# One engine per transposed block, identity products and one PSUM pool at the seam between image attention and the output stage

## The chip, the cores and the metric

The kernel runs on one core of one Trainium2 chip, in float32 throughout. The metric is the device time of one execution in microseconds (us). The engines are TensorE (PE, with its weight loads shown as PEld), VectorE (DVE), ScalarE (ACT), GpSimd (POOL) and SyncE (SP), which here only issues transfers. PE writes its results to PSUM, eight banks of 512 float32 values in each of 128 partitions; DVE and ACT copy them out from there to SBUF.

## The reference

Four layers, each applied to a group-normed copy of a tensor of 4 x 56 x 56 x 128 and added to it. Layers 0 and 1 are window and global attention with an MLP, and an edge layer. The change lies in layer 2, which treats every sample as a set of images, with an attention between them and spectral convolutions in each:

```python
x = x + _L0_conv_ref(_gn(x), ...)          # window attention, attention, MLP
x = x + _L1_conv_ref(_gn(x), ...)          # edge layer
x = x + _L2_conv_ref(_gn(x), ...)          # image attention and spectral layers
x = x + _L3_conv_ref(_gn(x), L3_conv_W, L3_conv_b)

# in layer 2
k = _fno_layer(xa_n, wK, wKs, bKs, (H // 2, W // 2))
q = _fno_layer(xa_n, wQ, wQs, bQs, (H // 2, W // 2))
v = _fno_layer(xa_n, wV, wVs, bVs, (H, W))
scores = jnp.einsum('bhtd,bhsd->bhts', qs, ks) / (np.sqrt(ks.shape[-1]) * TEMPERATURE)
attn_w = jax.nn.softmax(scores, axis=-1)
out = jnp.einsum('bhts,bhsd->bhtd', attn_w, vs)
projd = _fno_layer(out, wP, wPs, bPs, (H, W))
attention = _inorm(projd + xa, norm_g[1], norm_b[1])
an = _inorm(attention, norm_g[2], norm_b[2])
m = _fno_layer(an, wM0, wM0s, bM0s, (H, W), (norm_g[3], norm_b[3]), act=True)
m = _fno_layer(m, wM1, wM1s, bM1s, (H, W), (norm_g[4], norm_b[4]), act=False)
output = _inorm(m, norm_g[5], norm_b[5]) + attention
```

Here `_fno_layer` is a truncated two-dimensional Fourier transform, a product per mode, the inverse transform and a skip path, and `_inorm` normalizes an image.

## The kernel before

The whole computation is one program. Layers 0 and 1 run sample by sample (4 samples) until about 2700 us of the profile; then come the spectra and the score weights of layer 2, the image attention in `attend`, and the output stage in `outputs`, which does the rest of layer 2 and layer 3.

`attend` (L1802) works through 24 turns (g, n, bp): four groups g of eight spectral columns, three parts n of a complex product, two pairs bp of samples. In each turn DVE and POOL multiply a spectrum by coefficients (`u_ud`, `u_up`), PE multiplies with the attention weights `AT` into a bank `u_po` (L1874), and the result is copied or added into `st.y`, which has for each bp 32 columns c, each of 128 partitions (two samples of 64 images) by 2 x 56 values. After the last turn, two additions on DVE (L1901) finish the columns 24 to 31 of bp = 1. Those of bp = 0 are finished one turn earlier. `attend` holds its own PSUM pool: two buffers `u_px` of two banks, one `x_po` of two banks (for a part called `mix_images` and for the last softmax) and two of one bank for `u_po`.

`outputs` (L2630) opens a PSUM pool of its own: three buffers `o_d` of two banks each (`banks()`, tag d) and two `o_b` of one bank (`bank()`, tag b). A new pool gets the memory of the closed one, and work in it waits for what the old pool's buffers are still used for. The stage is described as a list of operations (`plan.add`), numbered in the order in which they are added, and issued in the order of the hand-written list OUTPUT_ORDER (L2598). Each engine takes its own instructions in that order. A sample is worked on in two halves of 28 images; (sample, half) is a unit, and two samples, so four units, share a bp.

`attended_rows` (L2569) is the seam. For each bp it turns the 32 columns of `st.y` in four blocks of eight: eight transpositions on PE into one `o_d` buffer (L2586), then four copies (L2593), one per unit, into the unit's rows `o_y` (112 partitions, 28 images, 32 columns). The copies of units with an odd number in the pair go to DVE, the others to ACT, so both engines read every block. Operations 0 to 19 are the four blocks of bp = 0 (0, 5, 10, 15 are the transpositions, for columns 0, 8, 16, 24; the four numbers after each are the copies), operations 20 to 39 those of bp = 1. The second group stands in the middle of the stage, after the first two samples have begun.

A unit then goes on in `half_sample` (L2067): `put_dc` (L2265, ACT) writes one row into `o_y`; `over_h` (L2114, PE) multiplies the rows with a transform, seven products a unit; `plain` (L2272, ACT) copies; `over_c` (L2131, PE) goes on; an addition (L2281, DVE) adds `o_a`, which SP has loaded from memory (L2260, four loads of 784 KB at the start of the stage); `over_w` (L2145), `weighted` (L2167, PE, then L2174, DVE) and so on, with norms and a gelu (L2336, ACT) between. `last_layer` does layer 3 per sample. The input of a sample for the last sums, `o_x`, is loaded (L2347) into memory that `st.y` leaves, so once all its rows are turned; `constant` (L2357, ACT) is the first to use it. `before_x`, the list of all copies, orders this load.

In the list, `put_dc` names all 16 copies of its bp and the load of `o_a` as operations that have to be issued before it. The waits on the chip are made from the buffers that the instructions touch, not from the list.

Of the kernel before, what the change touches and what calls it, by code (L numbers as in the profile page):

```python
# [12 lines left out]
F32 = mybir.dt.float32  # L13
# [3 lines left out]
PSUM = bass.MemoryType.PSUM  # L17
DRAM = bass.MemoryType.DRAM

P = 128  # L20
# [1780 lines left out]

def attend(k, I, w, st, dd, xat, xm, softmax, beside):  # L1802

    nc, tc = k.nc, k.tc
    with ExitStack() as es:
        mk = es.enter_context(tc.tile_pool(name="x_wk", bufs=1))
        dk = es.enter_context(tc.tile_pool(name="u_dk", bufs=3))
        wk = es.enter_context(tc.tile_pool(name="u_wk", bufs=2))  # L1810
        psum = es.enter_context(tc.tile_pool(name="u_ps", bufs=2, space=PSUM))

        def bank():
            return psum.tile([P, 2, 512], F32, name="x_po", bufs=1)

# [6 lines left out]
        def prepare(turn):  # L1822
            if turn == len(turns):
                return
            g, n, bp = turns[turn]
# [13 lines left out]
            else:  # L1839

                x, re = (st.xh[:, bs, i, cs, :].rearrange("p b c r -> p b (c r)") for i in (1, 0))
                nc.gpsimd.tensor_add(x, re, x)
            px = psum.tile([112, 2, 512], F32, name="u_px")
            nc.scalar.copy(px[:, :, :NB], x)
# [13 lines left out]
        for turn, (g, n, bp) in enumerate(turns):  # L1858
            cs = slice(8 * g, 8 * g + 8)
            x, px = ready.pop(turn)  # L1860
            po = psum.tile([P, 512], F32, tag="acc", name="u_po")
            left = 16
# [204 lines left out]
def half_sample(k, w, st, plan, b, half, whole, pools, rows, x2d, xm):  # L2067
# [4 lines left out]
    nc = k.nc  # L2072
    wk, psum = pools.wk, pools.psum
    T, G = HH // 2, HH // 8
# [12 lines left out]
    def bank():  # L2087
        return psum.tile([P, 512], F32, tag="b", name="o_b", bufs=2)

    def banks():  # L2090
        return psum.tile([P, 2, 512], F32, tag="d", name="o_d", bufs=3)

# [4 lines left out]
    def op(engine, cost, after=(), takes=(), gives=(), **kw):  # L2097
        return lambda run: plan.add(engine, cost, run, after, takes, gives, **kw)
# [162 lines left out]

    @op("ACT", 0.2, rows.ops + [load_a])
    def put_dc():
        V.y = rows.y[me]
        nc.scalar.copy(V.y[0:1, :, 0], st.dc[:, b, t0:t0 + T])  # L2265
# [169 lines left out]
def last_layer(k, w, plan, b, whole, pools, out):  # L2435


    nc = k.nc
    wk, psum = pools.wk, pools.psum
    V = Env()  # L2440
    count = [0]

    def buf(n):
        count[0] += 1
        return n, (b, count[0])

    def bank():
        return psum.tile([P, 512], F32, tag="b", name="o_b", bufs=2)

    def banks():  # L2450
        return psum.tile([P, 2, 512], F32, tag="d", name="o_d", bufs=3)

# [116 lines left out]
def attended_rows(k, st, plan, bp, pools):  # L2569

    nc = k.nc
    T = HH // 2
    rows = Env()
    rows.y, rows.ops, first = {}, [], []
    units = [(2 * bp + b2, half) for b2 in range(2) for half in range(2)]
    for c0 in range(0, 32, 8):
        d = "d", ("rows", bp, c0)
        L = Env()

        def turn(c0=c0, L=L):  # L2580
            if c0 == 0:
                for u in units:
                    rows.y[u] = pools.wk.tile([112, T, 32], F32, tag="y0", name="o_y0", bufs=4)
            L.pt = pools.psum.tile([P, 2, 512], F32, tag="d", name="o_d", bufs=3).rearrange("p i (c t) -> p (i c) t", c=4)
            for c in range(8):
                nc.tensor.transpose(L.pt[:112, c, :], st.y[:, bp, c0 + c].rearrange("p i r -> p (i r)"), k.ident)  # L2586
        p = plan.add("PE", 1.8, turn, first, [d] + ([("y0", u) for u in units] if c0 == 0 else []))
        first = first or [p]
        for i, (b, half) in enumerate(units):
            def copy_rows(i=i, b=b, half=half, c0=c0, L=L):  # L2590
                o = rows.y[b, half][:, :, c0:c0 + 8].rearrange("p t c -> p c t")
                at = 64 * (b % 2) + T * half
                (nc.vector.tensor_copy if i % 2 else nc.scalar.copy)(o, L.pt[:112, :, at:at + T])  # L2593
            rows.ops.append(plan.add("DVE" if i % 2 else "ACT", 0.4, copy_rows, [p], (), [d]))
    return rows


OUTPUT_ORDER = """  # L2598
# [30 lines left out]

def outputs(k, w, st, ys, x2d, xm, out):  # L2630

    tc = k.tc
    with ExitStack() as es:
        pools = Env()
        pools.wk = es.enter_context(tc.tile_pool(name="o_wk", bufs=2))
        pools.psum = es.enter_context(tc.tile_pool(name="o_ps", bufs=2, space=PSUM))
        opened = []

# [48 lines left out]
def build(k, packs, I, out):  # L2687
# [3 lines left out]
    with ExitStack() as es:  # L2691
# [100 lines left out]
        with tc.tile_pool(name="xh", bufs=1) as xp:  # L2792
            st.xh = xp.tile([112, B, 2, 32, HH], F32, name="xh")
            with tc.tile_pool(name="sp", bufs=1) as sp:
# [43 lines left out]
```

## Time and profile before

The time before is the median of three runs, 3626.33 us (3609.95 to 3628.69). The profile is of another execution.

| | value |
|---|---|
| time of the profiled execution | 3623.46 us |
| its span | 3621.7 us |
| mean granted TensorE clock | 0.973 |
| instructions | 80884 |
| attention products u_po (L1874), first to last | 2923.7 to 3253.6 us |
| output stage, first transposition to the end | 3255.4 to 3621.7 us |
| transpositions (L2586), records on PE | 64, of 272 ns each (median) |
| row copies (L2593) on ACT and on DVE | 16 of 552 ns and 16 of 534 ns (medians) |
| put_dc (L2265) | 8 of 232 ns |
| over_h (L2114), records on PE | 336, of 275 ns each (median) |
| last additions to y (L1901) | 2 of 618 ns |

How to read it: the page sums each engine's busy time over the span; the chain of waits follows the work that ended last back to the start, and gives each piece to an engine and a line. The timeline lists instructions of an engine with start, busy time, and in brackets how long the engine had been idle before and what ended that. A matmul's record is longer than its distance to the next, since matmuls are pipelined: the busy time of a row of them, divided by their number, says what one costs in a row. The windows sum busy time in stretches, with the granted clock of TensorE as a share of full speed. Transpositions and products carry one `MATMUL` and one `LDWEIGHTS` record or more each.

### The profile page before, as it was taken

To read this page: it belongs to the slowest core of one execution; us is meant where nothing else is said; L and a number is where in the kernel's file an instruction comes from. 1 tells how busy PE (TensorE), PEld (TensorE's weight loads), DVE (VectorE), ACT (ScalarE), POOL (GpSimd) and SP (SyncE) were. 2 spreads that over 40 slices of the span, in tenths; PEclk is the share of its full clock that TensorE was granted. 3 is DMA by queue.
4 is the path that set the end of the run, shared out by engine and by line. 5 is a ranking of instruction groups with operands and counts; after the bars stand their busy time and mean duration, and the time that the engine had idled before them with its cause. 6 is when DMAs were issued, how large, how long until landed. Compare 5 with 4: busy or idle time off the path is not lost.

```text
span 3621.7 us, 80884 instructions
## 1 busy us (share of the span) xinstructions
PE 3401.0 (94%) x36096; PEld 1567.0 (43%) x36096; DVE 2706.0 (75%) x2532; ACT 2091.6 (58%) x2103; POOL 1247.4 (34%) x751
## 2 busy tenths in 40 slices
PE   6999998999999898999989899999898989999998
PEld 4433344553333455333346543334466433336664
DVE  6588859758887786788859658885965768885756
ACT  4688865458887555788856468886542012215432
POOL 1000018500000660000038200001854768874766
PEclk9999999999999999999999999999998999999989
DMA  2243320024442002344400034332021047742201
GB/s 102 48 92 87 91 41 20 20 57 92 93 92 62 20 3 54 76 95 96 93 19 3 20 87 93 87 88 53 26 66 33 1 108 187 181 107 79 63 10 54
DMA packets 98496, 244.51 MB, mean 68 GB/s; under 512 B 64540, under 2 KB 69916, under 8 KB 93244
## 3 DMA queue, kind: packets, MB, share of 16 engines
q0 software_dynamic: 16128, 102.77, 14.0%
q1 hardware_dynamic: 75152, 123.61, 11.6%
q10 hardware_dynamic: 6860, 12.88, 1.3%
q8 instruction: 285, 4.67, 0.5%
q14 instruction: 71, 0.58, 0.0%
HBM read 79.46 MB, written 31.33 MB: 31 GB/s over the span
## 4 chain that ended last, share of the span: by engine, by line
PE 78%; DVE 10%; ACT 4%; issue 4%; POOL 3%; DMA 0%; DVEq 0%; POOLq 0%; SPq 0%; ACTq 0%
PE f_pm L818 17%; PE f_pm L684 15%; PE u_po L1874 8%; PE e_acc L1238 7%; PE q_acc L1732 3%; DVE e_td L1231 3%; PE f_pm L791 2%; PE e_po L1206 2%; PE f_pm L770 2%; ACT f_ring L821 1%; PE o_d L2548 1%; PE f_pm L464 1%; PE o_d L2145 1%; DVE f_acc L673 1%; PE f_pm L715 1%
## 5 line engine op out<-in xcount | busy, mean ns | idle before, releaser
L821 ACT ACTIVATE f_ring<-f_pm 128x1792 f32<-128x1792 f32 (+1 forms) x764 | 1093.9, 1482 | 228.6 <-PE f_pm L818 181.1
L673 DVE TENSOR_TENSOR f_acc<-f_acc,f_ring 128x1792 f32<-128x1792 f32 x468 | 947.7, 2025 | 191.1 <-ACT f_ring L821 160.9
L818 PE MATMUL f_pm<-f_qT,f_kT 32*128 32x448 f32 x5376 | 725.1, 571 | 15.5 <-ACT f_ring L821 5.1
L684 PE MATMUL f_pm<-f_ring,f_va 128*32 128x448 f32 (+1 forms) x6304 | 589.4, 490 | 0.0
L663 POOL DMA_DIRECT2D f_far<-f_ring x112 | 96.6, 862 | 1329.4 <-ACT f_ring L821 1087.9
L1231 DVE TENSOR_TENSOR e_td<-e_pa,e_c 128x1792 f32<-128x1792 f32 x252 | 491.1, 2018 | 14.1 <-ACT e_a L1196 14.1
L1233 POOL TENSOR_TENSOR e_tp<-e_a,e_c 128x1792 f32<-128x1792 f32 x140 | 451.5, 3263 | 101.5 <-PE e_acc L1238 60.0
L818 PEld LDWEIGHTS f_pm<-f_qT,f_kT 32*128 32x128 f32 x5376 | 260.0, 183 | 417.5 <-ACT f_ring L821 305.0
L1238 PE MATMUL e_acc<-e_td,t_shared 32*32 32x448 f32 x8064 | 325.9, 544 | 24.9 <-DVE e_td L1231 24.1
L684 PEld LDWEIGHTS f_pm<-f_ring,f_va 128*32 128x32 f32 x6304 | 163.8, 109 | 410.1 <-issue 397.8
L1869 DVE TENSOR_TENSOR u_ud<-u_px,u_d 112x1792 f32<-112x1792 f32 (+1 forms) x145 | 264.9, 1859 | 43.3 <-PE u_po L1874 35.9
L1235 ACT ACTIVATE e_tp<-e_tp 128x1792 f32<-128x1792 f32 x140 | 233.4, 1694 | 74.0 <-POOL e_tp L1233 74.0
L1871 POOL TENSOR_TENSOR u_up<-xh,u_d 112x1792 f32<-112x1792 f32 (+1 forms) x71 | 238.8, 3390 | 50.4 <-PE u_po L1874 36.3
L1238 PE MATMUL e_acc<-e_tp,t_shared 32*32 32x448 f32 x4480 | 222.8, 544 | 3.1 <-ACT e_tp L1235 2.4
L1874 PE MATMUL u_po<-u_ud,AT 112*64 112x448 f32 x1060 | 218.1, 549 | 6.4 <-issue 6.4
L1238 PEld LDWEIGHTS e_acc<-e_td,t_shared 32*32 32x32 f32 x8064 | 142.2, 103 | 138.5 <-DVE e_td L1231 79.5
L1874 PEld LDWEIGHTS u_po<-u_ud,AT 112*64 112x64 f32 x1060 | 75.6, 139 | 136.8 <-issue 122.5
L1717 POOL TENSOR_TENSOR q_u<-iS,q_g 128x1792 f32<-128x1792 f32 x32 | 102.8, 3236 | 64.9 <-PE s_px L1565 41.8
L1250 ACT COPY e_sums<-e_acc 128x1792 f32<-128x1792 f32 x28 | 46.3, 1652 | 136.4 <-PE e_acc L1238 136.4
L1238 PEld LDWEIGHTS e_acc<-e_tp,t_shared 32*32 32x32 f32 x4480 | 96.7, 103 | 52.9 <-issue 16.4
L728 DVE RECIPROCAL f_den<-f_den 128x448 f32<-128x448 f32 x28 | 82.6, 2951 | 44.1 <-ACT f_den L725 44.1
L1874 PE MATMUL u_po<-u_up,AT 112*64 112x448 f32 x476 | 105.1, 554 | 9.0 <-POOL u_up L1871 9.0
(525 smaller groups left out, 4557.0 us busy)
## 6 DMA issues: line engine op xcount, KB each, us to landing
f_far<-f_ring POOLq DMA_DIRECT2D x112, 896.0 KB, 6.3
u_d<-dd SPq DMA_DIRECT2D x44, 784.0 KB
f_far<-f_ring SPq DMA_DIRECT2D x28, 896.0 KB
xw<-in_x SPq DMA_DIRECT2D x4, 1568.0 KB
x2d<-x SPq DMA_DIRECT2D x4, 1568.0 KB
xat<-x SPq DMA_DIRECT2D x4, 1568.0 KB
x_xs<-xat ACTq DMA_DIRECT2D x32, 196.0 KB
xm<-x_ev ACTq DMA_DIRECT2D x64, 98.0 KB
```

The source lines that it names most:

```text
L673: nc.vector.tensor_add(e.acc, e.acc, slots(j, c))
L684: nc.tensor.matmul(e.po[heads[h], part], va[o, c, heads[h]], p, start=(c == 0), stop=(c == 23 and part.stop == NB))
L818: nc.tensor.matmul(ss[:, i, :NB], kT[heads[h], c * P:(c + 1) * P], qT[heads[h], blk(j)], start=True, stop=True)
L821: nc.scalar.activation(ring[:, slot:slot + m, :], ss[:, :m, :NB], AF.Exp, scale=scale)
L1231: nc.vector.tensor_tensor(t, am, cm, ALU.max)
L1233: nc.gpsimd.tensor_sub(t, bc(a.rearrange("p (l n) -> p l n", l=8), 1, 4), cm)
L1235: nc.scalar.activation(tf, tf, AF.Relu)
L1238: nc.tensor.matmul(acc[quarters[q], r, :NB], k.ident[o, o], t[o, q].rearrange("p l n -> p (l n)"), start=(g == 0), stop=(g == len(EDGE_TUR ...
L1732: nc.tensor.matmul(acc[bp][i][halves[hb % 2], hb // 2, :NB], x[o], u[o, 8 * hb:8 * hb + 8, :].rearrange("p h t -> p (h t)"), start=first, ...
L1869: nc.vector.tensor_mul(u, bc(px[:, :, :NB], 2, m), dm)
L1871: nc.gpsimd.tensor_mul(u, bc(x, 2, m), dm)
L1874: nc.tensor.matmul(po[64 * b2:64 * b2 + 64, :NB], st.AT[:, 8 * i + h0 + q, 2 * bp + b2, :], u[:, b2, q, :], start=(left == 16), stop=(left ...
```

## The change

- The transpositions `nc.tensor.transpose(out, in, ident)` become products `nc.tensor.matmul(out, in, ident)` of the same operands.
- A block is copied by one engine: for bp = 0, columns 8 and 24 by DVE and 0 and 16 by ACT; for bp = 1, columns 8 and 16 by DVE and 0 and 24 by ACT.
- `put_dc` of a unit names the four copies of its own unit (`rows.of[me]`) instead of all 16.
- OUTPUT_ORDER changes in two places: the first group's blocks are issued in the order 0, 5, 10, 15, their copies in order of their numbers, and each `put_dc` (41, 120, 228, 307) and the first `over_h` (42) stand between the last copies; in the second group the copies stand in order of their numbers. Transpositions of the second group keep their places.
- One PSUM pool is opened before `attend` and passed to `attend` and `outputs`. Its tags are px (two buffers of two banks), x (one of two banks) and b (two of one bank). `banks()` of the output stage goes round px, px, x; `bank()` is b, as `u_po` is.

```diff
-def attend(k, I, w, st, dd, xat, xm, softmax, beside):
+def attend(k, I, w, st, dd, xat, xm, softmax, beside, psum):
...
-        psum = es.enter_context(tc.tile_pool(name="u_ps", bufs=2, space=PSUM))
...
-            return psum.tile([P, 2, 512], F32, name="x_po", bufs=1)
+            return psum.tile([P, 2, 512], F32, tag="x", name="x_po", bufs=1)
...
-            px = psum.tile([112, 2, 512], F32, name="u_px")
+            px = psum.tile([P, 2, 512], F32, tag="px", name="u_px")[:112]
...
-            po = psum.tile([P, 512], F32, tag="acc", name="u_po")
+            po = psum.tile([P, 512], F32, tag="b", name="u_po")
...
-    @op("ACT", 0.2, rows.ops + [load_a])
+    @op("ACT", 0.2, rows.of[me] + [load_a])
     def put_dc():
...
+        dve = c0 in ((16, 8) if bp else (8, 24))
...
-            L.pt = pools.psum.tile([P, 2, 512], F32, tag="d", name="o_d", bufs=3).rearrange("p i (c t) -> p (i c) t", c=4)
+            L.pt = pools.banks().rearrange("p i (c t) -> p (i c) t", c=4)
             for c in range(8):
-                nc.tensor.transpose(L.pt[:112, c, :], st.y[:, bp, c0 + c].rearrange("p i r -> p (i r)"), k.ident)
+                nc.tensor.matmul(L.pt[:112, c, :], st.y[:, bp, c0 + c].rearrange("p i r -> p (i r)"), k.ident, start=True,
+                                 stop=True)
...
-                (nc.vector.tensor_copy if i % 2 else nc.scalar.copy)(o, L.pt[:112, :, at:at + T])
-            rows.ops.append(plan.add("DVE" if i % 2 else "ACT", 0.4, copy_rows, [p], (), [d]))
+                (nc.vector.tensor_copy if dve else nc.scalar.copy)(o, L.pt[:112, :, at:at + T])
+            rows.ops.append(plan.add("DVE" if dve else "ACT", 0.4, copy_rows, [p], (), [d]))
+            rows.of.setdefault((b, half), []).append(rows.ops[-1])
...
-0 40 119 227 306 10 3 2 1 4 5 13 12 11 14 15 6 9 7 8 18 19 16 17 41 228 120 42 307 121 43 45 44 122 124 229 47
+0 40 119 227 306 5 10 1 2 3 4 6 7 8 9 15 11 16 41 42 12 17 120 13 18 228 14 19 307 121 43 45 44 122 124 229 47
...
-239 73 149 147 74 76 240 20 150 247 25 24 23 22 21 248 77 35 29 27 30 28 37 36 39 26 38 82 31 32 33 34 78 151 83
+239 73 149 147 74 76 240 20 150 247 25 21 22 23 24 248 77 35 26 27 28 29 30 36 37 38 39 82 31 32 33 34 78
+151 83
...
-        pools.psum = es.enter_context(tc.tile_pool(name="o_ps", bufs=2, space=PSUM))
-        opened = []
+        opened, taken = [], [0]
+
+        def bank():
+            return psum.tile([P, 512], F32, tag="b", name="o_b")
+
+        def banks():
+            taken[0] += 1
+            tag, bufs = ("x", 1) if taken[0] % 3 == 0 else ("px", 2)
+            return psum.tile([P, 2, 512], F32, tag=tag, name="o_d", bufs=bufs)
+        pools.bank, pools.banks = bank, banks
...
-            attend(k, I, w2, st, dd, xat, xm, last_softmax, conv_weights(k, w2, l2p))
+            psum = es.enter_context(tc.tile_pool(name="l2_ps", bufs=2, space=PSUM))
+            attend(k, I, w2, st, dd, xat, xm, last_softmax, conv_weights(k, w2, l2p), psum)
...
-        outputs(k, w2, st, ys, x2d, xm, out)
+        outputs(k, w2, st, ys, x2d, xm, out, psum)
```

More of the change, by code (lines that the diff above doesn't have):

```diff
@@ L2072, in half_sample @@
     nc = k.nc
-    wk, psum = pools.wk, pools.psum
+    wk, bank, banks = pools.wk, pools.bank, pools.banks
     T, G = HH // 2, HH // 8
@@ L2085, in tile_of @@
         return wk.tile(shape, F32, tag=tag, name="o_" + tag, bufs=plan.buffers.get(tag, 6))
[L2087 to L2091, printed above, removed]
     def slots(x, i):
@@ L2438, in last_layer @@
     nc = k.nc
-    wk, psum = pools.wk, pools.psum
+    wk, bank, banks = pools.wk, pools.bank, pools.banks
     V = Env()
@@ L2445, in buf @@
         return n, (b, count[0])
[L2447 to L2451, printed above, removed]
     def tile_of(shape, tag):
@@ L2574, in attended_rows @@
     rows.y, rows.ops, first = {}, [], []
+    rows.of = {}
     units = [(2 * bp + b2, half) for b2 in range(2) for half in range(2)]
@@ L2583, in turn, with copy_rows @@
                     rows.y[u] = pools.wk.tile([112, T, 32], F32, tag="y0", name="o_y0", bufs=4)
-            L.pt = pools.psum.tile([P, 2, 512], F32, tag="d", name="o_d", bufs=3).rearrange("p i (c t) -> p (i c) t", c=4)
+            L.pt = pools.banks().rearrange("p i (c t) -> p (i c) t", c=4)
             for c in range(8):
-                nc.tensor.transpose(L.pt[:112, c, :], st.y[:, bp, c0 + c].rearrange("p i r -> p (i r)"), k.ident)
+                nc.tensor.matmul(L.pt[:112, c, :], st.y[:, bp, c0 + c].rearrange("p i r -> p (i r)"), k.ident, start=True,
+                                 stop=True)
         p = plan.add("PE", 1.8, turn, first, [d] + ([("y0", u) for u in units] if c0 == 0 else []))
         first = first or [p]
-        for i, (b, half) in enumerate(units):
-            def copy_rows(i=i, b=b, half=half, c0=c0, L=L):
+        for b, half in units:
+            def copy_rows(b=b, half=half, c0=c0, L=L, dve=dve):
                 o = rows.y[b, half][:, :, c0:c0 + 8].rearrange("p t c -> p c t")
                 at = 64 * (b % 2) + T * half
-                (nc.vector.tensor_copy if i % 2 else nc.scalar.copy)(o, L.pt[:112, :, at:at + T])
-            rows.ops.append(plan.add("DVE" if i % 2 else "ACT", 0.4, copy_rows, [p], (), [d]))
+                (nc.vector.tensor_copy if dve else nc.scalar.copy)(o, L.pt[:112, :, at:at + T])
+            rows.ops.append(plan.add("DVE" if dve else "ACT", 0.4, copy_rows, [p], (), [d]))
+            rows.of.setdefault((b, half), []).append(rows.ops[-1])
     return rows
 OUTPUT_ORDER = """
[1 row of a table removed]
[1 row of a table added]
 46 48 50 232 49 230 123 51 52 125 56 53 127 126 60 54 57 129 128 55 61 58 131 130 62 132 59 133 63 139 69 140 64
 134 141 65 135 142 66 80 67 70 136 68 75 231 137 71 308 233 148 138 234 235 143 236 72 144 311 309 145 158 146
[1 row of a table removed]
[2 rows of a table added]
 86 152 153 84 87 237 157 85 88 79 249 238 159 310 250 89 243 312 313 314 92 81 90 93 244 315 241 91 94 96 242
@@ L2627, with outputs @@
 """
-def outputs(k, w, st, ys, x2d, xm, out):
+def outputs(k, w, st, ys, x2d, xm, out, psum):
     tc = k.tc
```

## The prediction

> **What bounds the kernel now.** I read the page first: its table of busy time and its chain of waits. TensorE (PE) is busy in 94% of the span and holds 78% of the chain that ends last, so time is saved where PE waits or runs slowly.
>
> ```profile
> PE 3401.0 (94%) x36096; PEld 1567.0 (43%) x36096; DVE 2706.0 (75%) x2532; ACT 2091.6 (58%) x2103; POOL 1247.4 (34%) x751
> PE 78%; DVE 10%; ACT 4%; issue 4%; POOL 3%; DMA 0%; DVEq 0%; POOLq 0%; SPq 0%; ACTq 0%
> ```
>
> The change touches two places: the first seam (bp = 0, from 3254 us), and the second (bp = 1, at 3302 us), where the same four blocks are turned in the middle of the output stage. The timeline of the first, with gaps left out:
>
> ```profile
> 3254.14 1.15 DVE L1901 TENSOR_TENSOR y<-y,u_po 128x448 f32<-128x448 f32 x2 [3.23 <-PE u_po L1874]
> 3255.44 2.81 PE L2586 MATMUL o_d<-t_shared,y 128*112 128x128 f32 x24 [1.35 <-DVE y L1901]
> 3256.66 0.56 ACT L2593 COPY o_y<-o_d 112x224 f32<-112x224 f32 x1 [22.40 <-PE o_d L2586]
> 3257.25 0.55 DVE L2593 COPY o_y<-o_d 112x224 f32<-112x224 f32 x1 [1.95 <-ACT o_y L2593]
> 3257.83 0.91 ACT L2593 COPY o_y<-o_d 112x224 f32<-112x224 f32 x2 [0.62 <-DVE o_y L2593]
> 3259.07 1.06 PE L2586 MATMUL o_d<-t_shared,y 128*112 128x128 f32 x8 [0.83 <-DVE o_y L2593]
> 3263.37 6.28 PE L2114 MATMUL o_d<-t_images,o_y 112*128 112x112 f32 x28 [3.23 <-ACT o_y L2265]
> 3269.57 1.60 PE L2131 MATMUL o_d<-o_v,t_images 32*128 32x392 f32 x16
> 3271.10 1.81 PE L2114 MATMUL o_d<-t_images,o_y 112*128 112x112 f32 x14
> ```
>
> Three things are to be seen. PE waits 1.35 us for the last additions, though the bp = 0 blocks don't need them. ScalarE (ACT) and VectorE (DVE) copy a block by turns, each waiting for the other, never together. And the first 28 over-h products take 6.28 us where 14 of the same form later take 1.81. The windows say why the last (columns: time, length, busy time of each engine, granted clock, DMA share, GB/s):
>
> ```profile
> 3255.81:3262.64 6.83, 3.50 (x31) 3.04 (x29) 3.21 (x7) 3.29 (x7) 0.00 (x0) 1.00 1.30 230
> 3262.64:3269.47 6.83, 6.10 (x28) 6.05 (x28) 0.61 (x2) 1.77 (x7) 0.00 (x0) 0.50 1.31 218
> 3303.62:3310.45 6.83, 3.68 (x32) 3.19 (x30) 2.90 (x9) 5.85 (x11) 0.22 (x2) 1.00 0.38 121
> 3310.45:3317.28 6.83, 6.83 (x37) 5.01 (x36) 1.00 (x2) 3.39 (x4) 0.00 (x0) 0.50 1.01 432
> ```
>
> Each seam is a window in which PE works about half the time (3.50 and 3.68 us of 6.83), and the next window runs at half clock. The second seam shows the result in its timeline:
>
> ```profile
> 3302.21 2.79 PE L2586 MATMUL o_d<-t_shared,y 128*112 128x128 f32 x24
> 3305.81 1.08 PE L2586 MATMUL o_d<-t_shared,y 128*112 128x128 f32 x8 [0.81 <-ACT o_y L2593]
> 3309.23 5.17 PE L2145 MATMUL o_d<-t_images,o_t 128*128 128x64 f32 x28 [2.34 <-ACT o_y L2593]
> 3314.33 3.00 PE L2131 MATMUL o_d<-o_v,t_images 32*128 32x392 f32 x16
> ```
>
> **What the Trainium skill says.** TensorE: Matmul & The Clock Gate, Part 1: a free-running activity window halves PE's clock after an idle window; the trace agrees, though its falls here last 6.83 us and lie 7 x 6.83 apart. The same page, Part 4, says that transpose mode "doesn't count as PE-busy the same way"; the two falls fit, but don't prove it, since PE was idle half the time too (after 3.99 us of ordinary work, in the window from 2852.84, the clock fell as well). PSUM — Partial Sum Buffer, section PSUM bank collisions raise a hardware error: two engines may not read one bank and quadrant at once; the strict turns above are that rule put into waits. FP8 and Floating Point Precision, TensorE Precision Notes: a true FP32 product takes four passes. The trace shows two records for each product (168 over-h products in the code, 336 records) and one for each transposition (64, 64).
>
> **The change part by part.** Record time first. A transposition's is 2.81/24 = 0.117 us. A product of the same shape is not in the trace; nearest is over-h, whose weight loads pace it at 1.64/14 = 0.117 (14 loads, 1.64 us, full clock). Bounds are 0.108 (the loads of 112 columns, 2.59/24) and 0.129 (1.81/14 with its tail). I take 0.117, hence 2 x 0.117 x 8 = 1.87 us a block for 0.94 before: 7.5 us for four. Together 64 more records, 7.5 us of PE.
>
> *First seam.* With one pool the first product carries no wait in the built order; PE can start one slot (0.375 us, the spacing of pairs of u_po) after the last pair at 3253.55, at 3253.93. Blocks end at 3255.80, 3257.67, 3259.54 and 3261.42. From the end of a block to its first copy 0.28 us pass (3256.66 - 3255.44 - 0.94). The fourth block reuses the first one's bank: ACT's four copies, begun at 3256.08 and 0.37 us apart (three on DVE in 1.28), end at 3257.7, in time. ACT copies blocks one and three, DVE two and four; each copy row takes 0.53 to 0.56 alone. The first unit's over-h product waits for its own four copies and its put_dc instead of for all 16: last is DVE's first copy of block four, 3261.70 to 3262.23, so it starts at 3262.3, for 3263.37 before. Put_dc, spread between the last copies on ACT, costs 0.23 alone and 0.14 in a row; all four and the copies around them end about 3262.5, under over-h. DVE's last copies fall in its idle time before L2281 (7.39 us).
>
> So the copies' turns and the wait are worth 1.1 us net of the doubled products. The larger part is the clock: in the window to 3262.64 PE would be busy for 5.6 + 0.3 us, not 3.50. Then 28 records take 3.3 us, not 6.2, and over-c starts at 3265.6, for 3269.57: 4.0 us saved. The four loads o_a, issued at 3254.24, do not move. They move 3.1 MB at some 220 GB/s and end near 3269; the first addition moves from 3271.24 to 3267.3 and needs only the first load. If they were interleaved it would wait 2 us; I take nothing, since their issues follow each other by up to 3.8 us.
>
> *Second seam.* PE has no wait at 3302.21 today; four blocks end at 3309.70. Beneath them ACT does four copies (1.6), a table load (1.28) and a gelu (0.95), done by 3308.3; DVE's last four copies run under the next products. Over-w thus starts at 3309.70 for 3309.23, 0.5 us late. But at full clock it takes 3.2 and over-c 1.5 us (the same forms from 3320.45 and 3324.57), so L2167 starts at 3314.4 for 3317.26: 2.8 us saved. The x loads start when y is read out, so 2.8 us later than 3306.92; ACT's L2357, which needs the first, may slip from 3315.24 to about 3318 and end by 3321.2, and ACT's next work on the chain is due at 3324.16 - 2.8: hidden.
>
> Other edits cost nothing: px, x and b are as many banks as before, the three d banks still go round in turn (px, px, x), and instructions elsewhere keep their order.
>
> Sum: 4.0 + 2.8 = 6.8 us. The profiled execution took 3623.46 (span 3621.7 and 1.8 around it), so 3616.7; it lies 2.9 below the median of the runs, 3626.33. I predict **3619.5 us**.
>
> **Rivals.** *The clock falls all the same.* For it: one window with 5.57 us busy was followed by half clock. Against: its second half held only matmuls of 112 columns and of one, with gaps, while here the gap is 0.9 us between dense rows; windows with 5.40 and more at 3351 to 3379 kept full clock. It leaves 1.1 gained and 0.5 lost: 3625.7.
>
> *The long half-clock stretch is missed.* Late in the output stage stands this:
>
> ```profile
> 3453.88:3460.71 6.83, 5.57 (x42) 4.13 (x38) 4.94 (x10) 1.74 (x4) 6.37 (x5) 0.99 0.03 4
> 3460.71:3467.54 6.83, 6.62 (x30) 3.00 (x34) 4.09 (x9) 1.29 (x6) 1.09 (x1) 0.50 0.00 0
> 3488.03:3494.86 6.83, 6.83 (x29) 5.36 (x30) 1.16 (x2) 4.64 (x4) 0.00 (x0) 0.51 0.00 0
> 3494.86:3501.69 6.83, 6.83 (x64) 4.69 (x60) 2.33 (x3) 1.50 (x2) 3.50 (x2) 1.00 0.00 1
> ```
>
> 34 us at half clock after one gap of 1.2 us cost up to 17 us. The runs, 3626, 3629 and 3610, look as if one had escaped it. If the moved work usually escapes: 3602.4.
>
> *Slower: a second such stretch.* Place: the last sample, from 3550 us, where windows hold 5.75, 6.37, 4.84 and 5.51 us of PE and the clock fell once, briefly. If the 6.8 us shift drops a gap there across a window while small matmuls follow, another 17 us is lost: 3636.6. It decides from the point where a window there falls under about 5.6 us with small matmuls after it. Against: the stage's order is unchanged. That the pool doesn't remove the wait is ruled out by the built order.
>
> **How the numbers follow.** Forecast 0.52, clock falls 0.20, stretch missed 0.20, second stretch 0.08. Unknown costs are product records (0.7 us each way at each seam), loads (2 us) and which half-clock windows a run meets (5 to 10 us); the range, 3602 to 3633, reaches the missed stretch and leaves most of the second out. About 0.5% (18 us) is what a measurement of this kernel tells from no change. Beyond it on the fast side lies the third case alone, 0.20; slower than 3644.5 needs the fourth and more, 0.05; 0.75 is left between.
>
> **What would show it.** Products with 128 records, not 64, and a first start near 3253.9; four copies in a row on one engine, without turns; over-h starting near 3262.3 and taking 3.3 to 3.5 us for 28; full clock in both windows after the seams; L2167 of the second seam some 6.8 us earlier. It is wrong if products cost more than 0.13 a record, if the clock halves after either seam, or if the first o_t addition waits for its load.

## The result and the profile after

The changed kernel takes 3606.95 us (median of 17 runs, 3602.56 to 3614.25), the kernel before, beside it, 3624.11 us (17 runs, 3607.35 to 3630.09): a ratio of 0.9967, with an interval of 0.9954 to 0.998. The medians lie 17.2 us apart, but the times of the kernel before fall into two groups: eight runs up to 3616 us, nine from 3624 to 3630. All times of the changed kernel lie beside or below the lower group, whose median, 3611.4, is 4.4 us above its own. So there are two questions: what the seams gained, and why the upper group is gone.

The timeline of TensorE (PE) at the first seam of the changed kernel (start, busy time, engine, line, operation, count of records, and in brackets the idle time before and what ended it):

```profile
3258.04 3.18 PE L1873 MATMUL u_po<-u_ud,AT 112*64 112x448 f32 x16
3261.15 7.24 PE L2575 MATMUL o_d<-t_shared,y 128*112 128x128 f32 x64
3269.06 3.35 PE L2107 MATMUL o_d<-t_images,o_y 112*128 112x112 f32 x28 [0.67 <-ACT o_y L2583]
3272.34 1.60 PE L2124 MATMUL o_d<-o_v,t_images 32*128 32x392 f32 x16
```

The first product follows the attention products with no wait, where 1.35 us stood. All 32 products run in one row, 64 records in 7.24 us, so 0.113 us each. Over-h waits 0.67 us for 3.23, and its 28 records take 3.35 us for 6.28.

ScalarE (ACT) and VectorE (DVE) in the same stretch, two answers of the timeline:

```profile
3263.30 1.72 ACT L2583 COPY o_y<-o_d 112x224 f32<-112x224 f32 x4 [21.92 <-PE o_d L2575]
```

```profile
3264.93 1.71 DVE L2583 COPY o_y<-o_d 112x224 f32<-112x224 f32 x4 [2.51 <-PE o_d L2575]
3274.01 1.85 DVE L2274 TENSOR_TENSOR o_t<-o_a,o_d 128x784 f32<-128x784 f32 x2 [3.90 <-PE o_d L2124]
```

Each block is four copies in a row, and what ends their idle time is PE, no longer the other copying engine. The last additions to y, 1.15 us from 3261.26, run beside the first products. The first o_t addition waits for over-c, not for the load of o_a.

The second seam on PE, without over-c, and below it what ACT does after it:

```profile
3304.97 7.15 PE L2575 MATMUL o_d<-t_shared,y 128*112 128x128 f32 x64
3311.96 3.24 PE L2138 MATMUL o_d<-t_images,o_t 128*128 128x64 f32 x28
...
3316.66 3.26 PE L2160 MATMUL o_d<-o_z,t_images 56*112 56x448 f32 x16
```

```profile
3319.92 3.10 ACT L2350 ACTIVATE o_x<-o_x,factors 128x1568 f32<-128x1568 f32 x2 [3.78 <-DMA o_x<-x2d]
3323.28 0.91 ACT L2144 COPY o_z<-o_d 128x896 f32<-128x896 f32 x1 [0.27 <-PE o_d L2138]
```

PE has no gap at all here (over-c fills the 1.6 us left out). The x load comes later, and ACT waits 3.78 us for it, but its next copy still waits 0.27 us for PE: the delay ends where nobody asks for it.

The windows of the changed kernel (time, length, busy time of PE, PEld, DVE, ACT and POOL, granted clock, DMA share, GB/s), at the two seams and at the late place of the long half-clock stretch:

```profile
3261.12:3267.95 6.83, 6.83 (x64) 6.81 (x63) 2.86 (x6) 2.99 (x10) 0.73 (x3) 1.00 1.00 184
3310.83:3317.66 6.83, 6.83 (x62) 5.57 (x62) 2.55 (x5) 2.57 (x6) 0.22 (x2) 1.00 0.65 230
3460.33:3467.16 6.83, 6.10 (x53) 3.86 (x53) 5.50 (x10) 2.08 (x7) 2.26 (x2) 1.00 0.01 2
```

The clock is 1.00 in all of them, and by the trace's clock records it stays so from the seams until 3541 us; the windows of before had 0.50 after both seams, and from 3460.71 to 3494.86. The gap that stood ahead of that stretch is still there, 1.23 us for 1.20:

```profile
3461.06 0.59 PE L2191 MATMUL o_b<-o_t,c_ones 112*32 112x224 f32 x8 [1.23 <-ACT o_t L2180]
```

The two profiled spans, 3621.7 and 3609.0 us, can be split at starts that stand in both timelines:

| part | before | after | difference |
|---|---|---|---|
| up to the last row of 16 u_po products | 3250.92 | 3258.04 | +7.1 |
| first seam: from there to over-c | 18.65 | 14.30 | -4.35 |
| over-c to the last over-h row ahead of the second group | 30.99 | 30.98 | 0.0 |
| second seam: from there to `weighted` (L2167, now L2160) | 16.70 | 13.34 | -3.36 |
| to the end of the late gap | 143.66 | 144.40 | +0.7 |
| to the end of the span | 160.78 | 147.94 | -12.8 |

The first row is no effect of the change that these runs can show: over the fourteen profiles taken here, of which four are of the kernel before or built on it, that start lies anywhere from 3250.4 to 3258.3 us, and the changed kernel's own second profile has it at 3253.44. The seams are 7.7 us shorter. The largest part is the last row, where the stretch of before is missing. That row holds other falls too: between the gap and the last 10 us the clock is at half for 44.4 us in before, the stretch included, and for 17.1 us in the changed kernel. Half of the difference, 13.7 us, is near the 12.8 us of the row.

### The profile page after: what moved, and what is told of

It is laid out like the page before. It is cut to its first block, busy times and chain, and to the rows that moved or that the text cites. A ratio compares the mean times of both kernels' runs of the same rounds, so it can differ in the third digit from the quotient of the medians.

```text
span 3609.0 us, 81008 instructions
## 1 busy us (share of the span) xinstructions
PE 3394.6 (94%) x36160; PEld 1561.9 (43%) x36160; DVE 2704.4 (75%) x2532; ACT 2090.1 (58%) x2103; POOL 1247.6 (35%) x751
## 4 chain that ended last, share of the span: by engine, by line
PE 79%; DVE 10%; issue 4%; ACT 4%; POOL 2%; DMA 0%; DVEq 0%; POOLq 0%; ACTq 0%; SPq 0%
PE f_pm L818 17%; PE f_pm L684 15%; PE u_po L1873 8%; PE e_acc L1238 7%; PE q_acc L1732 3%; DVE e_td L1231 3%; PE f_pm L791 2%; PE e_po L1206 2%; PE f_pm L770 2%; ACT f_ring L821 1%; PE o_d L2535 1%; PE f_pm L464 1%; PE o_d L2138 1%; PE o_d L2160 1%; DVE f_acc L673 1%
```

## The experiments

Below, "first seam" and "second seam" are the distances of the second and fourth row of that table. The first expectations count from the last pair of u_po products, which is 2.7 us less for the first seam. Each kernel was timed beside the kernel before on the same chip, in three series; the medians of before were 3609.91, 3614.37 and 3615.79 us. The first four rows of the table are the first series, the next four the second, the last four the third. The last column counts the times above 3621 us, where the upper group is taken to begin; in the second and third series no time of before lies from 3619 to 3623, but in the first there are 3620.0 and 3621.5, so there the cut is less sharp.

| kernel | first seam | second seam | median us (runs) | ratio to before, interval | over 3621 us |
|---|---|---|---|---|---|
| b_products | 17.00 | 14.19 | 3608.72 (22) | 0.9988 (0.9978 to 0.9998) | 0 |
| a_two_pools | 15.69 | 13.33 | 3604.68 (22) | 0.998 (0.9968 to 0.9992) | 0 |
| a_transpose_twice | 14.25 | 13.33 | 3604.68 (22) | 0.9976 (0.9965 to 0.9988) | 0 |
| a_transpose | 11.16 | 15.79 | 3598.75 (12) | 0.9958 (0.9942 to 0.9974) | 0 |
| after_again | 14.30 | 13.33 | 3606.92 (22) | 0.9975 (0.9966 to 0.9984) | 0 |
| a_copies | 12.56 | 11.97 | 3606.01 (21) | 0.997 (0.9959 to 0.998) | 0 |
| a_shift8 | 14.30 | 13.34 | 3606.18 (19) | 0.9972 (0.9961 to 0.9983) | 0 |
| b_shift4 | 18.64 | 16.71 | 3616.37 (22) | 0.9998 (0.9986 to 1.0009) | 4 |
| before_again | 18.69 | 17.46 | 3619.48 (14) | 1.0011 (0.9997 to 1.0025) | 7 |
| a_late | 22.26 | 17.38 | 3619.17 (14) | 1.0005 (0.9993 to 1.0017) | 2 |
| a_transpose_again | 11.16 | 11.97 | 3601.59 (7) | 0.9956 (0.9938 to 0.9975) | 0 |
| a_mixed | 11.17 | 13.34 | 3603.11 (10) | 0.9968 (0.9956 to 0.9981) | 0 |

### Which part does what: products, transpositions, pool

a_transpose is the changed kernel with transpositions again:

```diff
-                nc.tensor.matmul(L.pt[:112, c, :], ..., k.ident, start=True, stop=True)
+                nc.tensor.transpose(L.pt[:112, c, :], ..., k.ident)
```

> The changed kernel with transpositions in place of the identity products; everything else as changed. Theory (transpositions don't keep the clock up): TensorE falls to half clock in a window after each seam, as before, which gives back about what the 64 missing records save (7.2 us of PE), so the distance from the last attention product to over-c (11.6 us in the changed kernel) comes out at 10.5 to 12 and the whole time within 3 us of the changed kernel, more where the long half-clock stretch returns. Rival (only idle time lowers the clock, and the copies by one engine are what shortened it): no fall at the first seam, that distance near 8.1 us, and the time 5 to 7 us below the changed kernel.

a_transpose_twice issues each of these transpositions two times:

```diff
+                for _ in range(2):
+                    nc.tensor.transpose(L.pt[:112, c, :], ..., k.ident)
```

> The changed kernel with every identity product replaced by the same transposition issued twice, so that PE has the same 128 records, of the same shape, at the seams. Theory (transpositions don't count as activity): half clock after both seams, 3 us lost at each, 6 to 7 us slower than the changed kernel, and more if the long stretch returns. Rival (only idle time counts): no fall, the same time as the changed kernel within 1 us.

PE at the two seams of a_transpose, the first row of blocks and over-h, then the last block and over-w of the second:

```profile
3258.24 2.83 PE L2575 MATMUL o_d<-t_shared,y 128*112 128x128 f32 x24
3263.01 3.35 PE L2107 MATMUL o_d<-t_images,o_y 112*128 112x112 f32 x28 [0.67 <-issue]
...
3302.41 1.08 PE L2575 MATMUL o_d<-t_shared,y 128*112 128x128 f32 x8 [0.70 <-ACT o_y L2582]
3304.67 5.53 PE L2138 MATMUL o_d<-t_images,o_t 128*128 128x64 f32 x26 [1.01 <-ACT o_t L2329]
```

At the first seam the clock holds (28 over-h records in 3.35 us), as the rival had it, and the seam is 3.1 us shorter than with products. At the second PE catches up with ACT, waits 0.70 and 1.01 us, and the clock falls (26 over-w records in 5.53 us), as the theory had it. Doubled transpositions leave no such gap; the row of a_transpose_twice:

```profile
3255.88 7.20 PE L2576 MATMUL o_d<-t_shared,y 128*112 128x128 f32 x64
```

This is the changed kernel's row to 0.04 us. In its 7.20 us PE does nothing but transpositions. The clock's records in this trace change on a grid of 3.41 us, so that a row of more than two such lengths holds a whole interval of the grid, and no fall follows at either seam. The theory that transpositions don't keep the clock up is out; what the falls at these seams go with is gaps on PE. In the same series a_transpose, with half of these records, has a median 5.9 us lower (3598.75 and 3604.68).

a_two_pools opens a PSUM pool for each stage again; b_products is the kernel before with the products alone.

```diff
-            psum = es.enter_context(tc.tile_pool(name="l2_ps", bufs=2, space=PSUM))
-            attend(...)
+            with tc.tile_pool(name="l2_ps", bufs=2, space=PSUM) as psum:
+                attend(...)
...
+        psum = es.enter_context(tc.tile_pool(name="o_ps", bufs=2, space=PSUM))
```

> The changed kernel with a PSUM pool of its own for attend and one for the output stage, as before. The first product waits again for the last additions: its idle time before the first block is 1.3 to 1.5 us instead of none, and the time rises by 1.1 to 1.4 us. Rival (the one pool carries most of the gain): 4 us or more slower.

> The kernel before with identity products in place of transpositions, and nothing else. Theory (clock): full clock after both seams though the copies still take turns; 4 to 6 us faster than the kernel before in its quicker runs (3611), and over-c some 14.3 us after the last attention product for 16.0 before. Rival (copies and waits): the products only add to PE, so no gain or 2 to 4 us slower, and the clock falls all the same.

PE at the first seam, the row of blocks of a_two_pools, then over-h of b_products:

```profile
3262.80 7.21 PE L2575 MATMUL o_d<-t_shared,y 128*112 128x128 f32 x64 [1.34 <-DVE y L1900]
```

```profile
3268.31 3.38 PE L2114 MATMUL o_d<-t_images,o_y 112*128 112x112 f32 x28 [1.96 <-ACT o_y L2265]
```

The second pool costs its wait for y, 1.34 us, and the seam is 1.4 us longer; the second seam, which lies inside one pool, doesn't change. Its median is level with a_transpose_twice's (3604.68 both), so that the 1.4 us don't show in it. In b_products the copies still take turns, and over-h waits 1.96 us for them, where it waited 3.23, and no fall follows: 28 records take 3.38 us. So the doubled records did fill part of the gap of the kernel before. They are one way to do so. The expected gain in time did not come: the two seams are 4.2 us shorter than before's, but the median is level with that of the lower times of before in that series (3608.72 and 3608.8), and no run here says where the 4 us went. What the products did take away is the upper group, 0 of 22 for 13 of 65.

### One engine per block alone

a_copies is the kernel before with the copies and the order of the change (`put_dc`'s four copies included), but transpositions and two pools: a_transpose and a_two_pools in one. With it went the changed kernel once more.

> The kernel before with one part of the change alone: each transposed block copied out by one engine, and the order that goes with it; transpositions and two PSUM pools stay. Theory (the copies' turns are what held TensorE back; the pool is worth 1.4 us of idle TensorE; the products buy nothing): from the last u_po pair to over_c 8.4 + 1.4 = 9.8 us, no fall at the first seam, median 4 to 8 us below the lower group of the before runs and below the changed kernel's by 1 to 4 us. Rival (the clock at the first seam is kept by the products or by the pool, not by the copies): a fall of 6.8 us at the seam, 12 us or more to over_c, and a median not below the changed kernel's.

> The changed kernel once more, so that the variants have it beside them. Theory (each seam is cheaper by 3 to 4.5 us, and the rest of the median's gain is that the upper group of the before kernel's times, some 14 to 17 us above the lower, is absent): median 4 to 5 us below the lower group of the before runs, none of its times above 3618 us; no fall of the clock within 15 us of either seam. Rival (the whole 17 us is work that the change removes from every run): its median is 15 us or more below the lower group too.

PE at the first seam of a_copies, from the first block on:

```profile
3262.80 2.81 PE L2575 MATMUL o_d<-t_shared,y 128*112 128x128 f32 x24 [1.35 <-DVE y L1900]
3265.80 1.08 PE L2575 MATMUL o_d<-t_shared,y 128*112 128x128 f32 x8 [0.19 <-ACT o_y L2582]
3267.56 3.35 PE L2107 MATMUL o_d<-t_images,o_y 112*128 112x112 f32 x28 [0.67 <-issue]
```

Here is the main part of the change. The bank for the fourth block comes 0.19 us late, not 0.83, over-h waits 0.67 us, not 3.23, and the clock holds: 12.56 us for 18.65, so 6.1 us saved, of which 2.9 are over-h at full clock (3.35 for 6.28). Which of the two does it, one engine per block or the order that comes with it, is not shown: neither was run alone, and the shorter wait of over-h can owe something to a `put_dc` that no longer stands behind all 16 copies. Its median is 0.9 us below the changed kernel's in the same series, where 1 to 4 was expected; the intervals overlap, so that this alone doesn't rank the two. The changed kernel again shows no time above 3613 us; its median is 5.9 us below that of the 53 lower times of before in this series.

### Is it the arrival at the late gap?

The theory was that the seam moves the late gap against the clock's grid. Repeats of one product after both seams move the gap and change nothing else, 8 in the changed kernel (a_shift8) and 4 in the kernel before (b_shift4):

```diff
+            V.turn = getattr(V, "turn", 0) + 1
-            for g in range(G):
+            for g in [0] * (8 if (me, V.turn) == ((0, 0), 3) else 0) + list(range(G)):
```

> The changed kernel with 8 repeats of the first 112-column product in the third over_h of the first unit, after both seams: 1.9 us of added TensorE work and a later arrival at the gap ahead of L2191. Theory (a boundary of the clock's 3.41 us windows just before the end of that gap starts a half-clock stretch of some 34 us): 1.9 us later the boundary falls about 0.4 us before the gap's end, the stretch appears there in most runs, and the median is 14 to 18 us above the changed kernel's. Rival (the stretch isn't decided by the arrival time): median 1 to 3 us above the changed kernel's, no stretch of over 20 us after 3440 us in the profile.

> The kernel before with 4 such repeats, 0.94 us of added TensorE work after both seams and nothing else. Theory (phase against the clock's windows decides the upper group): the boundary moves to some 1.2 us before the gap's end, the upper group disappears, and the median is about 1 us above the lower group of the before runs, so level with or below the before runs' median if these have the upper group. Rival (the arrival doesn't decide it): the share of times in the upper group is as in the before runs of the same call, and the median 1 us above theirs.

Both missed. a_shift8 has no time above 3612.1 us and is level with the changed kernel (0.7 below it, with 1.9 us more work, which says how much a median of some 20 runs is worth here). b_shift4 keeps the upper group, 4 of 22 for 18 of 71 of before. A fixed arrival against the grid, as the theory had it, doesn't explain the group.

But the shifts don't settle the arrival itself. The grid is not tied to the program: worked back in steps of 3.41 us from the last fall of each trace, the last step before the gap's end lies 0.30 us ahead of it in before and 2.73 us in before_again, which is the same kernel; it lies 1.97 us ahead in the changed kernel and 1.91 in a_shift8, which was to move it by 1.9. The gap, of 1.15 to 1.23 us, stands in eleven of the fourteen profiles. A step falls inside it in before alone, and there the stretch follows; in the other ten it lies 1.22 to 2.73 us ahead of the gap's end, and the clock holds. Two intervals of the grid with all or most of the gap in them, of before (with the interval after it) and of before_again (columns as above), have the same busy time of PE, and half clock follows the first alone:

```profile
3457.21:3460.62 3.41, 2.23 (x19) 1.91 (x17) 1.61 (x7) 1.57 (x3) 3.12 (x4) 1.00 0.02 5
3460.62:3464.03 3.41, 3.11 (x14) 1.28 (x16) 1.86 (x6) 1.12 (x5) 0.00 (x0) 0.50 0.00 0
```

```profile
3465.09:3468.50 3.41, 2.23 (x24) 1.69 (x25) 0.90 (x7) 1.70 (x5) 2.14 (x3) 1.00 0.02 5
```

So an arrival that differs from execution to execution stays possible, with one profile for it. In the other three profiles (after_again, a_transpose_twice, a_mixed) the clock falls earlier, between 3432 and 3436 us, for 10.2 to 17.1 us, and the gap isn't there.

### Does a fall at the seam bring the upper group?

a_late makes PE idle at both seams of the changed kernel, by repeating one copy:

```diff
-                (nc.vector.tensor_copy if dve else nc.scalar.copy)(o, L.pt[:112, :, at:at + T])
+                for _ in range(10 if c0 == 24 and (b % 2, half) == (0, 0) else 1):
+                    (nc.vector.tensor_copy if dve else nc.scalar.copy)(o, L.pt[:112, :, at:at + T])
```

> The changed kernel with the first row copy of each seam's last block done ten times, so that TensorE waits some 4 us more ahead of over_h and of its counterpart at the second seam. Theory (idle TensorE at the seams makes the clock fall there, and executions with these falls are the ones that can go into the upper group): a fall of 3.4 to 10.3 us at one or both seams, the median 8 to 14 us above the changed kernel's, and some of its times 12 us or more above its lower group. Rival (the upper group comes from something else that the change took away): the median as said, with no second group.

> The kernel before once more, as a control and for a second trace of it. Theory (its times fall into two groups because its half-clock windows differ from execution to execution): about a quarter of its times above 3618 us, ratio within 0.998 to 1.002; falls of the clock at both seams in the profile whichever group it is in; a stretch of over 20 us near 3460 us only if the profiled time is above 3618 us. Rival (the two groups aren't a matter of the clock's stretch near 3460 us): a profiled time above 3618 us without it, or one below with it.

Over-h at the first seam of a_late, then its windows there:

```profile
3266.66 6.11 PE L2107 MATMUL o_d<-t_images,o_y 112*128 112x112 f32 x28 [5.88 <-DMA o_a<-xm]
```

```profile
3262.22:3265.63 3.41, 0.00 (x0) 0.00 (x0) 3.20 (x7) 0.00 (x0) 0.00 (x0) 1.00 1.25 215
3265.63:3272.46 6.83, 5.79 (x27) 5.83 (x28) 1.94 (x5) 0.87 (x2) 0.00 (x0) 0.50 0.64 121
```

The line names a load as the end of the wait, but the trace's list of who waits for whom has over-h's weight load waiting 6.0 us for DVE's repeated copies, the tenth of which begins at 3265.93 and takes 0.53 us. The wait leaves one interval with nothing on PE, and half clock follows. So the fall can be made at will with an idle stretch, with the products in place, and it costs 2.8 us in over-h (6.11 for 3.35). The median rose by some 11 us (ratio 1.0005 for 0.9975 of the changed kernel), as expected. But its times lie between 3613.9 and 3624.3 without a gap; the two above 3621 are the end of one group, and the highest lies 10.4 us above the lowest. In these 14 runs the falls at the seam alone don't bring the upper group.

before_again has 7 of 14 times in the upper group, where a quarter was expected, and was profiled in an execution of 3612.08 us, so in the lower one. PE at its first seam and at the late gap, then a window that holds the gap:

```profile
3267.22 6.31 PE L2114 MATMUL o_d<-t_images,o_y 112*128 112x112 f32 x28 [3.24 <-ACT o_y L2265]
...
3467.82 0.59 PE L2198 MATMUL o_b<-o_t,c_ones 112*32 112x224 f32 x8 [1.19 <-ACT o_t L2187]
```

```profile
3462.80:3469.60 6.80, 5.35 (x46) 4.04 (x45) 4.15 (x13) 2.39 (x6) 4.43 (x4) 1.00 0.01 2
```

The seam has the same waits and the same fall, and the late gap is the same, but eight records after it take 0.59 us and not 0.98: no stretch. From the gap's end to the span's end it takes 142.5 us (3610.3 - 3467.82), 18.3 less than the first profile. That is somewhat more than the distance of the two groups' medians, 13.5 to 17.3 us in the four series, and the first profile has 10.2 us more at half clock after the stretch, near 3556 and 3570 us. The clock of each run bears the reading out: of the 182 runs of before in the three series, the 45 above 3621 us had a mean granted clock of 0.972 (0.968 to 0.974), the 137 others 0.976 (0.973 to 0.979). A difference of 0.0042 over 3615 us is, by an estimate from these figures, 30 us more at half clock. So the upper group is a matter of half clock, about as much as the long stretch has (34.1 us); that it is this stretch each time rests on one profile of each kind. a_late's two times above 3621 us had 0.974 and 0.975.

### Back to transpositions

a_mixed has transpositions at the first seam and products at the second:

```diff
+                if bp == 0:
+                    nc.tensor.transpose(L.pt[:112, c, :], ..., k.ident)
+                else:
                     nc.tensor.matmul(L.pt[:112, c, :], ..., k.ident, start=True, stop=True)
```

> The changed kernel with transpositions in place of the products at both seams, once more. Theory (at the first seam the transpositions save 3 us and the clock holds; at the second it falls and takes most of that back): median 2 to 5 us below the changed kernel's of the last call (ratio to before 0.995 to 0.998), with a fall of the clock at the second seam and none at the first. Rival (its lower time in the first call was chance): ratio 0.998 or above.

> The changed kernel with transpositions at the first seam and products at the second. Theory (each seam has the form that is cheaper there): from the last u_po pair to over_c 8.4 us as with transpositions, from the last L2107 group to L2160's counterpart at the second seam 13.3 us as with products, no fall at either, and the median 3 us below the changed kernel's and 1 to 3 us below that of transpositions at both. Rival (the records of the products at the first seam are what holds the clock, and the one profile without a fall was luck): a fall at the first seam and a median level with the changed kernel's.

Over-w at the second seam of a_transpose_again:

```profile
3305.59 3.12 PE L2138 MATMUL o_d<-t_images,o_t 128*128 128x64 f32 x26 [1.00 <-ACT o_t L2329]
```

The waits are those of a_transpose (0.70 us ahead of the last block, 1.00 here), yet the clock holds this time (3.12 us for 5.53), as in a_copies: the expected fall came in one of three profiles. The place of the grid differs (the emptiest interval there had 1.71 us of PE in a_transpose, 1.79 in the two others), and so the same waits don't always bring the fall, and transpositions are cheaper at this seam too, by 1.4 us when it doesn't come. a_mixed did at both seams what was expected, but was not below the kernel with transpositions at both (ratios 0.9968 and 0.9956, intervals overlapping); its profile is of its slowest run. Of what was run, the change with one pool and one engine per block, but with transpositions, has the lowest medians: 0.9958 and 0.9956 of before in two series, against 0.9967 and 0.9975 for the changed kernel in two others. They were not timed in one series, and the intervals touch; that it beats the changed kernel rests on these four ratios, on the 5.9 us to a_transpose_twice and on seams that are 4.5 us shorter without the fall (23.1 us for 27.6).

## Why the prediction was right, and where it was not

- *No wait ahead of the first product.* Right: 3261.15, at the end of the row of u_po. a_two_pools prices the pool at 1.4 us.
- *Record time 0.117 us.* A little high: 7.24 / 64 = 0.113, and 0.112 at the second seam. Hence over-h came 8.3 us after the last u_po pair (3260.78 to 3269.06), 0.5 earlier than worked out, and the second seam's over-w was not 0.5 us late but level: 6.99 us after the block's start, for 7.02.
- *Copies, put_dc, banks, the loads of o_a.* As described. The profile names ACT as what over-h waited for, but ACT's last copy ends at 3268.64; DVE's first copy of block four, which had been named, begins at 3268.42, takes 0.53 us and so ends 0.1 us before over-h starts.
- *The clock stays up after both seams.* Right in both profiles of the changed kernel. The reason was not quite right: the windows of 6.83 us in which PE worked about half the time are two steps of the grid each, and the falls of before follow the second step, with 0.90 and 1.21 us of PE in 3.41. Nor were these steps idle, so the trace agrees with an idle window less well than the prediction says. What the Trainium skill's page TensorE: Matmul & The Clock Gate, Part 4, says of transpositions, that they don't count as busy in the same way, had been set beside the falls without being relied on; a_transpose_twice shows that in this kernel they hold the clock as products do (7.20 us of them and no fall), and the measurement decides.
- *First seam 4.0 us.* 4.35. *Second seam 2.8 us.* 3.36, with ACT's use of x slipping by 1.9 us after the block's start (14.95 for 13.03) and hidden, with 0.27 us to spare.
- *Other edits cost nothing.* The 31 us between the seams are equal. The 0.7 us lost between the second seam and the late gap come with the copies and their order: that stretch is 143.66 us in before and 143.59 in b_products, but 144.40 in the changed kernel, 144.37 in a_copies and 144.39 in a_transpose_again. What in them costs it is not shown.
- *The sum.* 6.8 us were forecast, the seams gave 7.7, and against the lower group of before the median moved by 4.4 and 5.9 us, 3.3 and 1.8 us less than the seams, of which the 0.7 us above are a part and the rest is open. But the predicted time, 3619.5, was 12.6 us too high (3606.95); it lies inside the range because the range was drawn to reach the missed stretch. The step that failed is the base: the sum was set against an execution with the long half-clock stretch and left that stretch in place. "The long half-clock stretch is missed" stood among the rivals at 0.20, at 3602.4 us, and it is what happened: none of 39 runs of the changed kernel shows the upper group, and of the kernel before 54 of 199.
- *The size of that stretch* was given as up to 17 us; 18.3 us separate the two profiles of before after the gap, the two short falls near 3556 and 3570 us included, and 13.5 to 17.3 us the groups.
- *Second stretch, clock falling all the same:* neither appeared.

Why the stretch is missed is not settled. The upper group comes in executions of the two kernels with copies by turns and falls at both seams, before and b_shift4. It is absent from 22 runs of b_products, which has the same copies and no falls in its profile, and from all variants of the changed kernel. That points to the falls. Against them stands a_late, which has falls and, in 14 runs, no second group; at the rate of before that would happen in about one of a hundred cases (145/199 to the power 14). a_transpose, with a fall at the second seam in one of two profiles, has no time above 3607 us in 19 runs either. The arrival at the gap, as worked out from one profile each, did not bring or remove the group in the two shifts, but the traces show that it changes from execution to execution by itself, so what decides it, the seams' falls among others, is untested.

## What to carry to other kernels

When two engines read out blocks of one PSUM bank by turns, give each a block of its own: that, with the issue order that goes with it, took 6.1 us from a seam here, half of it because TensorE's idle time no longer led to half clock. A product in place of a transposition is not needed for the clock where the gaps are gone, and costs its second record. Before setting a gain against one profiled time, look at whether the runs fall into groups, and which group the profile is of: here the upper group's absence is worth 13.5 to 17.3 us and the seams 7.7.

## What the runs showed of the hardware

- The clock falls and rises on a grid of 3.41 us. In the fourteen profiles from 3200 us on, all 37 returns to full clock follow an interval in which PE was busy throughout (3.41 us); but intervals as full were also followed by more half clock, in the long stretch and at the seams of before.
- No share of busy time decides the fall: at the seams intervals with 0.00 to 2.14 us of PE led to it, elsewhere intervals with 1.70 us didn't, and of two with 2.23 us at the late gap one did (before) and one didn't (before_again). In after_again an interval that was busy throughout led to it, as its windows show, and so did one each in a_mixed and a_transpose_twice:

```profile
3429.50:3432.92 3.42, 3.42 (x32) 3.38 (x31) 2.76 (x7) 3.39 (x6) 3.42 (x3) 1.00 0.03 3
3432.92:3436.33 3.41, 3.41 (x14) 1.92 (x13) 3.41 (x4) 1.15 (x3) 3.41 (x2) 0.50 1.16 230
```

- A float32 transposition and a record of a product of the same shape cost alike (7.20 and 7.24 us for 64 in a row); the product needs two.
